# Loading half of the tap weights behind x, and giving the first products of layer 0 banks of their own

## Chip, cores and metric

One core of a Trainium2 chip runs the whole program. The metric is device time in microseconds, the median of several executions; lower is better. The engines are TensorE (PE, with its weight loads as PEld), VectorE (DVE), ScalarE (ACT), GpSimd (POOL) and SyncE (SP, which here only issues DMAs).

## The reference, cut to what matters

The model has two residual layers on an image of 64 x 64 positions with 96 channels. The change touches layer 0 alone. Inside it, the part in question is the input projection, the depthwise 3 x 3 convolution with SiLU, and the first steps of a selective scan in four directions:

```
x = x + L0(groupnorm(x))
x = x + L1(groupnorm(x))

L0(x):
    xz = x @ in_proj_w                    # 96 -> 2 * 192
    x_val, z = xz[..., :192], xz[..., 192:]
    xc = depthwise_conv3x3(x_val) + conv_b
    u = silu(xc)                          # 64 x 64 x 192
    y = scan(u by rows) + scan(reversed) + scan(u by columns) + scan(reversed)
    y = layernorm(y) * silu(z)
    return y @ out_proj_w

scan(u):
    x_dbl = u @ x_proj_w                  # dt (6), B (16), C (16)
    dt = softplus(x_dbl[dt] @ dt_proj_w + dt_proj_b)
    decay = exp(cumsum(dt * A))
    h = decay * cumsum(dt * B * u / (decay + 1e-12))
    return sum_n(h * C) + u * D_skip
```

## The kernel before

**Layout.** Channels lie on partitions, positions along the free axis. The 192 inner channels make two tiles: tile 0 has channels 0 to 127, tile 1 the other 64, which appear twice so that the two halves of the partitions hold two stretches of positions. The image is cut into 8 blocks of 512 positions (`NCH`) and 4 chunks of 1024 (`NSC`). In the scan of layer 0 the factor `decay` falls so fast that only the first positions of each direction contribute (the windows, at most 160 of 192 steps `WT`); the rest of the image needs only the convolution, SiLU and a scaling with `D_skip`.

**Tile 0** folds the projection and the convolution into one matrix product. `load_taps` allocates `wi` (the projection's weights) and `cw` (the nine taps, broadcast to 96 partitions and for both tiles, 2 x 128 columns each). `load_cw` issues the load of `cw` on ACT's queue. In `front`, two GpSimd products (taps 0 to 4 and 5 to 8) turn `cw` into tap times projection weight. A block of convolved output is then nine accumulated matmuls with `cw[:, j, 0:P]` on shifted views of `pad`, the normalized image with a border of zeros. Only these first 128 columns of `cw` are read by a matmul.

**Tile 1** projects first and convolves afterwards: `depthwise` has PE make `px` (helper `project`), ACT copies it to `xz` (chunks 0 and 1) or `xz_later` (chunks 2 and 3), and DVE adds up nine taps per chunk with `scalar_tensor_tensor`, two chunks in turn.

**Order.** All instructions of layer 0 go through the class `Ordered`, which chains those of each engine in program order; its line, L373, is therefore the line of nearly every row of the profile. What order the engines see is thus the order in which the Python code calls them. `run` first loads (`load_x` puts two quarters of `x` on ACT's queue and two on SP's), then calls `front`: 32 transposes on PE into PSUM tiles `pt`, BN statistics on DVE and copies to `x1` on ACT, the group norm's mean and deviation with small products on PE and some products `warm` between them, and the normalization into `pad` and, for the outermost columns, `edge`. DVE does `pad` of block 0, both `edge` parts and `pad` of blocks 1, 2, 4 and 6; ACT does blocks 7, 3 and 5.

Then comes `window_inputs`: the products `pxw` of rows and columns at the image's edges for tile 1 (two matmuls each, in the two halves of a PSUM tile), copied by ACT to `window_work` and convolved by DVE; the products `pw` of tile 0 for the same positions, rows first and then columns; and SiLU of both into `uw`. From here three generators are advanced by a list of steps written out by hand in `run`: `depth` (tile 1), `conv` (tile 0: three matmuls per step, and a finished block `pc` evicted by ACT in the middle of the next) and `work`, which is `windows`: `pdw` (the `x_proj` product, two halves), `dblw` copied out and stored, `pvw` (the product with `dt_proj_w`, two tiles), the logarithm of softplus by quadratics (`wq`, `wacc`), the gates by Exp and Sigmoid, the rows of B and C reloaded from DRAM (`wB`, `wC`), one scan per tile and the sum `wy`. After the list the generators run in turn, joined by `finish`, which applies SiLU and the scaling to each chunk as soon as it is convolved. Layer norm, gating with `z` and the output projection follow, then layer 1.

**PSUM** has eight banks here: `px` and `pv` (two banks each), `wp` (one) and `conv` (three of one bank). Before, `pxw` uses `px` for the rows and `pv` for the columns, every `px` of `depthwise` uses `px`, both `pdw` use `wp`, and both `pvw` use `pv`. A tile that is handed out again under the same tag can be written only when its earlier readers are done.

Of the kernel before, what the change touches and what calls it, by code (L numbers as in the profile page):

```python
# [11 lines left out]
F32 = mybir.dt.float32  # L12
BF16 = mybir.dt.bfloat16
AF = mybir.ActivationFunctionType
ALU = mybir.AluOpType
# [5 lines left out]
C = 96  # L21
# [3 lines left out]
E = R + 2 * NS  # L25
P = 128
# [360 lines left out]
class Layer0:  # L387
# [24 lines left out]
    def load_taps(self, sb):  # L412
        nc = self.nc
        self.wi = sb.tile([C, 2 * P], F32, name="wi_0")
        nc.sync.dma_start(self.wi, self.w_in)
        self.cw = sb.tile([C, 9, 2 * P], F32, name="cw_0")

    def load_cw(self):

        self.nc.scalar.dma_start(  # L420
            self.cw.rearrange("p k d -> p (k d)"),
            self.conv_w.rearrange("o k d -> o (k d)").to_broadcast([C, 9 * 2 * P]),
        )
# [13 lines left out]
    def front(self, sb, ps):  # L437
# [4 lines left out]
        for b in range(NCH):  # L442
            pt = ps.tile([C, NB // P, P], F32, tag="tr", bufs=4, name=f"pt_{b}")
            for j in range(NB // P):
                nc.tensor.transpose(pt[:, j, :], self.xt[:, b * (NB // P) + j, :], k["ident"])
            nc.vector.bn_stats(stats[:, b, :], pt.rearrange("c j p -> c (j p)"))
            nc.scalar.copy(
                free(x1, (n, P), (1, NB // P), at=b * (NB // P)),
                free(pt, (1, P), (P, NB // P)),
            )  # L450
            if b == 0:
                self.load_cw()
        for some in (slice(0, 5), slice(5, 9)):
            n = some.stop - some.start
            at = self.cw[:, some, :]
            nc.gpsimd.tensor_tensor(at, at, free(self.wi, (0, n), (1, 2 * P)), ALU.mult)

# [34 lines left out]
    def window_inputs(self, sb, ps):  # L492
# [8 lines left out]
        for cols in range(2):  # L501
            px = ps.tile([P, 2, NB], F32, tag=("px", "pv")[cols], name=f"pxw_{cols}")
            for i, first in enumerate((0, side)):
                lines = (side, 2)[i]
# [11 lines left out]
                at = 2 * (cols * n + first * (W + 2))  # L516
                nc.scalar.copy(xw[:, at : at + width], px[:, i, 0:width])
        depth = self.depthwise(self.conv_sb, ps)
# [18 lines left out]
        for cols in range(2):  # L537
            pw = ps.tile([P, 2, side, H], F32, tag="conv", bufs=3, name=f"pw_{cols}")
            for j in range(9):
# [9 lines left out]
                nc.tensor.matmul(pw, self.cw[:, j, 0:P], at, start=(j == 0), stop=(j == 8))  # L549
            if cols == 0:  # L550
                next(depth)
            for back in range(2):
# [51 lines left out]
    def depthwise(self, sb, ps):  # L604
# [4 lines left out]
        def project(c):  # L609
            px = ps.tile([P, 2, NB], F32, tag="px", name=f"px_{c}")  # L610
            for i in range(2):
# [14 lines left out]
        for c in range(2):  # L626
            xz.append(project(c))
            yield

# [6 lines left out]
        for pair in range(0, NSC, 2):  # L636
            for j in range(9):
                for c in range(pair, pair + 2):
# [7 lines left out]
                    else:  # L646
                        nc.vector.scalar_tensor_tensor(
                            out, at, self.taps[:, j : j + 1], out, ALU.mult, ALU.add
                        )
                if j in (4, 8) and len(xz) < NSC:  # L650
                    xz.append(project(len(xz)))
# [27 lines left out]
    def windows(self, sb, ps):  # L679
# [10 lines left out]
        for h in range(2):  # L690
            pd = free(
                ps.tile([P, NB], F32, tag="wp", name=f"pdw_{h}")[0:E, :], (WT, 2), (1, WT)
            )
# [9 lines left out]
        for t in range(2):  # L703
            pv = ps.tile([P, 2, NB], F32, tag="pv", name=f"pvw_{t}")
            for h in range(2):
# [404 lines left out]
    def run(self, load):  # L1110
        nc, tc, side = self.nc, self.tc, WT // H
        with ExitStack() as st:
# [8 lines left out]
            with tc.tile_pool(name="front0", bufs=1) as fr, tc.tile_pool(  # L1121
# [8 lines left out]
                nc.gpsimd.memset(self.edge, 0.0)  # L1130
                nc.gpsimd.memset(self.zero, 0.0)
                self.load_later(res, sb)
                self.front(fr, ps)
                next(load)
# [8 lines left out]
            for step in (  # L1143
                depth, work, depth, conv, work, work, depth, conv, work, depth, conv, depth,
                work, conv, work, work, conv, work, work,
            ):
                next(step)
# [933 lines left out]
```

## Time and profile before

| what | us |
|---|---|
| median of three runs | 605.26 (604.91 to 607.9) |
| the profiled execution's own time | 603.7 |
| its span on the core | 602.0 |
| busy in the span: PE / DVE / ACT / POOL | 497.4 / 506.5 / 323.0 / 357.7 |
| busy from 16 to 124 us: PE / DVE / ACT / POOL | 101.84 / 86.71 / 58.88 / 20.64 |
| first product `pxw` starts | 17.33 |
| layer 1 begins (its load of tap weights is issued) | 171.3 |

The times within the profile count from the start of the span. A row of the timeline gives start, duration, engine, source line and instruction with `out<-in`, the shape, the number of instructions merged into the row, and in brackets how long the engine had been idle before the row and what it was waiting for. A row of the table of stages gives a stretch, its length, the busy time of PE, PEld, DVE, ACT and POOL with the number of instructions, the clock that PE was granted (1.00 is full speed), the share of the DMA engines that was busy, and GB/s.

### The profile page before, as it was taken

The numbers are of one execution on the slowest core, as the hardware profiler recorded it, in microseconds if no ns is written. First come the engines' busy times: TensorE is split into PE (matmuls) and PEld (weight loads), VectorE is DVE, ScalarE is ACT, GpSimd is POOL, SyncE is SP. The second block draws the span as 40 slices with busy tenths as digits, with TensorE's granted clock in tenths as the row PEclk, the third lists the DMA queues.
The fourth block names the chain that finished last, engine by engine and source line by source line (L and its number), as shares of the span: only waits on it lengthen the run. The fifth ranks groups of instructions, "written<-read, shape, count | busy, mean of one in ns | idle before, by whom it ended". The sixth has DMA issues, their size and how long they took to land.

```text
span 602.0 us, 4796 instructions
## 1 busy us (share of the span) xinstructions
PE 497.4 (83%) x1363; PEld 196.9 (33%) x1363; DVE 506.5 (84%) x465; ACT 323.0 (54%) x491; POOL 357.7 (59%) x205
## 2 busy tenths in 40 slices
PE   5798999997988997995689987878997566998583
PEld 3253444535842332331113322112332101433111
DVE  6974899934851899999999999999899999899991
ACT  5325599358834857582576765275665335333410
POOL 5326010003420298866697879888787896689961
PEclk9688799997999799996779989787997967897967
DMA  6100730000010816762675637674565585465911
GB/s 178 31 2 10 211 123 0 0 1 1 2 26 13 240 62 182 251 178 72 145 231 172 211 114 175 164 215 145 183 195 144 138 213 193 139 233 176 223 41 33
DMA packets 29734, 76.20 MB, mean 127 GB/s; under 512 B 10880, under 2 KB 11292, under 8 KB 29346
## 3 DMA queue, kind: packets, MB, share of 16 engines
q1 hardware_dynamic: 29186, 73.83, 42.5%
q10 hardware_dynamic: 512, 1.97, 1.1%
q8 instruction: 13, 0.21, 0.1%
q14 instruction: 23, 0.19, 0.1%
HBM read 69.37 MB, written 2.25 MB: 119 GB/s over the span
## 4 chain that ended last, share of the span: by engine, by line
DVE 37%; PE 20%; issue 8%; ACT 5%; POOL 1%; DMA 1%; DVEq 0%; POOLq 0%; ACTq 0%; SPq 0%
DVE h L373 20%; PE y L373 9%; DVE f L373 8%; DVE acc L373 5%; PE f L373 2%; PE pd L373 2%; PE po L373 2%; ACT f L373 2%; PE pv L373 1%; ACT q L373 1%; DVE dt L373 1%; PE f_pc L373 1%; ACT e L373 1%; ACT dA L373 1%; PE f_pd L373 1%
## 5 line engine op out<-in xcount | busy, mean ns | idle before, releaser
L373 POOL TENSOR_TENSOR C<-C,h 128x1024 f32<-128x1024 f32 x96 | 233.2, 2441 | 41.6 <-issue 14.3
L373 DVE TENSOR_TENSOR_SCAN h<-dA,last,f 128x1024 f32<-128x1024 f32 x57 | 133.8, 2347 | 7.5
L373 PE MATMUL y<-C,ident 128*128 128x512 f32 x256 | 131.6, 637 | 6.6 <-POOL C L373 6.4
L373 DVE TENSOR_TENSOR f<-f,w 128x1024 f32<-128x1024 f32 x76 | 92.2, 1214 | 6.3 <-PE f L373 5.9
L373 PE MATMUL f<-parts,pick 96*128 96x512 bf16 x144 | 49.1, 426 | 49.3 <-DVE h L373 49.3
L373 ACT ACTIVATE dA<-dt,A 128x1024 f32<-128x1024 f32 x76 | 86.3, 1143 | 3.1 <-DVE h L373 1.6
L373 PEld LDWEIGHTS y<-C,ident 128*128 128x128 f32 x256 | 50.1, 201 | 62.5 <-issue 42.4
L373 PE MATMUL pc<-pad,cw 96*128 96x512 f32 (+1 forms) x144 | 62.1, 594 | 0.0
L373 PE MATMUL y<-C,both 128*64 128x512 f32 x128 | 47.9, 841 | 7.6 <-POOL C L373 7.6
L373 POOL TENSOR_TENSOR B<-B,w 128x1024 f32<-128x1024 f32 x20 | 47.6, 2378 | 1.2 <-DMA B<-bc_dram 1.1
L373 ACT COPY last<-h 128x1 f32<-128x1 f32 x72 | 13.5, 187 | 64.4 <-DVE h L373 64.3
L373 PEld LDWEIGHTS <-pick 96*128 96x128 bf16 x144 | 10.3, 100 | 109.6 <-DVE h L373 68.1
L373 DVE TENSOR_TENSOR_SCAN h<-dA,f 128x1024 f32<-128x1024 f32 x19 | 43.4, 2286 | 2.2
L373 ACT ACTIVATE q<-e,quad 128x512 f32<-128x512 f32 (+1 forms) x24 | 27.3, 1145 | 31.2 <-DVE acc L373 30.9
L373 DVE SCALAR_TENSOR_TENSOR acc<-q,acc 128x512 f32<-128x512 f32 (+1 forms) x18 | 42.7, 2370 | 1.6 <-ACT q L373 1.3
L373 ACT ACTIVATE f<-dt,A 128x1024 f32<-128x1024 f32 x20 | 22.3, 1114 | 35.3 <-DVE h L373 26.9
L373 PEld LDWEIGHTS pc<-pad,cw 96*128 96x128 f32 x144 | 29.2, 206 | 32.5 <-issue 30.7
L373 PE MATMUL pc<-xn,cw 96*64 96x512 f32 (+1 forms) x84 | 33.5, 684 | 5.1 <-ACT u L373 4.8
L373 DVE TENSOR_TENSOR_SCAN h<-f,last,B 128x1024 f32<-128x1024 f32 x15 | 35.0, 2332 | 0.0
L373 POOL TENSOR_TENSOR rest<-dbl,parts 96x1024 f32<-96x1024 f32 (+1 forms) x5 | 11.1, 2215 | 37.9 <-ACT parts L373 37.8
L373 POOL TENSOR_SCALAR ln_small<-ln_small 128x4 f32<-128x4 f32 x2 | 0.5, 235 | 52.4 <-DVE ln_small L373 52.4
L373 ACT ACT_TABLE_LOAD x17 | 21.8, 1283 | 2.0 <-PEq L2071 1.7
(212 smaller groups left out, 732.5 us busy)
## 6 DMA issues: line engine op xcount, KB each, us to landing
C<-bc_dram SPq DMA_DIRECT2D x64, 512.0 KB, 3.9
C<-bc_dram SPq DMA_DIRECT2D x64, 256.0 KB, 4.2
B<-bc_dram SPq DMA_DIRECT2D x12, 512.0 KB, 5.4
B<-bc_dram SPq DMA_DIRECT2D x16, 256.0 KB, 4.4
dt<-dt SPq DMA_DIRECT2D x16, 128.0 KB, 2.3
w<-w SPq DMA_DIRECT2D x16, 128.0 KB, 2.3
wB<-rows_dram SPq DMA_DIRECT2D x1, 1472.0 KB
wC<-rows_dram SPq DMA_DIRECT2D x1, 1472.0 KB
```

The source lines that it names most:

```text
L373: ins = it(*args, **kw)
```

## The change

`cw` keeps only tile 0's half, 9 taps of 128 columns, loaded with nine pieces of 128 values for each partition; the load is issued before `load_later`, that is, ahead of `front`, and one GpSimd product follows there instead of two in `front`. In `window_inputs` both matmuls of a `pxw` tile come before both copies. The four `px` of `depthwise` take the tags `px` and `pv` in turn, the second `pdw` takes a `conv` bank, and the two `pvw` take `px` and `pv`. `depthwise` projects chunks 0 and 1 in one step, ahead of `pw`, and chunks 2 and 3 together after tap 4 of the first pair; `depth` then has one step more in the list and is advanced in other places. In the order of instructions on the engines this moves one `px` of PE ahead of the first `pw`, one ahead of the first `pc`, with it the copy of the last `xz_later` on ACT ahead of `pvw`'s readers, and four of DVE's taps on `xz_later` ahead of `wacc`.

```diff
@@ load_taps, load_cw
-        self.cw = sb.tile([C, 9, 2 * P], F32, name="cw_0")
+        self.cw = sb.tile([C, 9, P], F32, name="cw_0")
...
+        w = self.conv_w
         self.nc.scalar.dma_start(
-            self.cw.rearrange("p k d -> p (k d)"),
-            self.conv_w.rearrange("o k d -> o (k d)").to_broadcast([C, 9 * 2 * P]),
+            self.cw, bass.AP(w.tensor, w.offset, [[0, C], [2 * P, 9], [1, P]])
         )
@@ front
-            if b == 0:
-                self.load_cw()
-        for some in (slice(0, 5), slice(5, 9)):
-            n = some.stop - some.start
-            at = self.cw[:, some, :]
-            nc.gpsimd.tensor_tensor(at, at, free(self.wi, (0, n), (1, 2 * P)), ALU.mult)
@@ window_inputs
+            copies = []
             for i, first in enumerate((0, side)):
...
-                nc.scalar.copy(xw[:, at : at + width], px[:, i, 0:width])
+                copies.append((xw[:, at : at + width], px[:, i, 0:width]))
+            for to, of in copies:
+                nc.scalar.copy(to, of)
...
-            if cols == 0:
-                next(depth)
@@ depthwise
-            px = ps.tile([P, 2, NB], F32, tag="px", name=f"px_{c}")
+            px = ps.tile([P, 2, NB], F32, tag=("px", "pv")[c % 2], name=f"px_{c}")
...
         for c in range(2):
             xz.append(project(c))
-            yield
+        yield
...
-                if j in (4, 8) and len(xz) < NSC:
+                while j == 4 and len(xz) < NSC:
                     xz.append(project(len(xz)))
@@ windows
-                ps.tile([P, NB], F32, tag="wp", name=f"pdw_{h}")[0:E, :], (WT, 2), (1, WT)
+                ps.tile(
+                    [P, NB], F32, tag=("wp", "conv")[h], bufs=(1, 3)[h], name=f"pdw_{h}"
+                )[0:E, :], (WT, 2), (1, WT)
...
-            pv = ps.tile([P, 2, NB], F32, tag="pv", name=f"pvw_{t}")
+            pv = ps.tile([P, 2, NB], F32, tag=("px", "pv")[t], name=f"pvw_{t}")
@@ run
+                self.load_cw()
                 self.load_later(res, sb)
+                nc.gpsimd.tensor_tensor(
+                    self.cw, self.cw, free(self.wi, (0, 9), (1, P)), ALU.mult
+                )
                 self.front(fr, ps)
...
             for step in (
-                depth, work, depth, conv, work, work, depth, conv, work, depth, conv, depth,
-                work, conv, work, work, conv, work, work,
+                depth, work, depth, conv, work, work, conv, depth, work, depth, conv, depth,
+                depth, work, conv, work, work, conv, work, work,
             ):
```

## The prediction

> **What bounds the kernel now.** All of the change lies in layer 0, which ends near 172 us of a span of 602.0 in the profiled execution. So I first asked the timeline which engine carries layer 0 from the first products (17.3 us) to the end of the convolution. The last lines of that stage, ACT and then DVE:
>
> ```profile
> 119.03 0.69 ACT L373 ACTIVATE v<-pc,vec 128x512 f32<-128x512 f32 x1 [3.73 <-PE pc L373]
> 123.87 0.53 ACT L373 ACTIVATE v<-pc,vec 128x320 f32<-128x320 f32 x1 [4.16 <-PE pc L373]
> 126.76 2.39 DVE L373 TENSOR_TENSOR v<-v,wy 128x192 f32<-128x192 f32 x8 [7.08 <-ACT v L373]
> ```
>
> Columns: start, duration (us), engine, instruction, then in brackets the idle time before it and what ended it. DVE sat idle for 7.08 us until ACT had finished the last chunk, and ACT had waited 4.16 us for PE's last convolution product `pc`. Everything after hangs on that point: PE's convolution sets it, not the window scans on DVE (done at 119.7). Next the table of stages on core 0, with PE's granted clock behind POOL's column:
>
> ```profile
> 17.20:20.60 3.40, 1.64 (x5) 0.59 (x4) 3.40 (x2) 2.11 (x4) 3.40 (x2) 1.00 0.32 66
> 20.60:24.00 3.40, 1.66 (x2) 0.50 (x2) 3.40 (x6) 0.01 (x1) 1.29 (x1) 0.53 0.16 35
> 24.00:34.20 10.20, 9.67 (x20) 4.63 (x21) 9.54 (x17) 1.57 (x3) 0.00 (x0) 0.50 0.01 2
> 34.20:51.30 17.10, 16.54 (x59) 7.43 (x57) 13.43 (x21) 6.11 (x13) 9.98 (x15) 0.99 0.01 3
> 51.30:54.90 3.60, 2.03 (x8) 1.19 (x8) 0.00 (x0) 1.48 (x2) 3.38 (x5) 1.00 0.04 18
> 54.90:68.30 13.40, 13.40 (x27) 6.34 (x26) 5.44 (x9) 7.84 (x10) 0.00 (x0) 0.50 0.31 74
> 68.30:102.90 34.60, 34.60 (x81) 15.11 (x80) 33.93 (x37) 32.37 (x64) 1.63 (x10) 1.00 0.36 117
> ```
>
> PE is busy nearly throughout, but in two stretches, 20.6 to 34.2 and 54.9 to 68.3, at a clock of 0.50. Each follows a stretch of about 3.5 us in which PE worked only half the time (1.64 of 3.40, 2.03 of 3.60). The same matmul shows it: eighteen `pw` records take 9.20 us from 28.1, mostly in the first stretch, and 6.08 us from 38.5. So a short wait of PE costs here several times its own length. The waits themselves:
>
> ```profile
> 16.59 5.56 DVE L373 TENSOR_SCALAR edge<-x,mean,rstd 96x256 f32<-96x256 f32 x2
> ...
> 18.98 0.71 PE L373 MATMUL pxw<-pad,wi 96*128 96x264 f32 x2 [0.74 <-ACT window_work L373]
> ...
> 22.30 1.66 PE L373 MATMUL pxw<-edge,wi 96*128 96x396 f32 x2 [2.60 <-DVE edge L373]
> ...
> 24.53 1.25 PE L373 MATMUL pxw<-edge,wi 96*128 96x264 f32 x2 [0.58 <-ACT window_work L373]
> ...
> 46.67 1.60 PE L373 MATMUL pdw<-uw,w_x 128*38 128x384 f32 x4 [0.56 <-ACT dblw L373]
> ...
> 54.19 1.82 PE L373 MATMUL pvw<-dblw,dtw 6*128 6x320 f32 x4 [1.57 <-ACT wdt L373]
> ```
>
> The second `pxw` product waits for the copy of the first, though it fills another half of the tile; the second `pdw` and `pvw` wait for the readers of their predecessor's tile. The 2.60 us belong to `edge`: two DVE operations on 256 elements in 5.56 us, where `pad` with 512 takes 0.54. POOL's product with the tap weights runs beside them (16.24 to 21.88, in two records of 3.18 and 2.51), and each `edge` record (3.10 and 2.55) ends about 0.27 us after one of POOL's. And one long wait on DVE:
>
> ```profile
> 62.70 0.55 DVE L373 TENSOR_SCALAR v<-xz_later,taps,vec 128x512 f32<-128x512 f32 x1 [11.46 <-ACT xz_later L373]
> ```
>
> **What the Trainium skill says.** "SBUF — State Buffer", section "SBUF: two separate sides": DVE and GpSimd share a port pair, an exclusive lock held for a whole instruction, taken by DVE operations in a two-port mode or with two SBUF inputs. The `edge` durations agree. BN statistics read from PSUM should be free of it, and the trace agrees: eight of them at 0.61 us each beside nothing, and later 4 in 1.14 us beside a POOL product (155.84, POOL busy 155.43 to 157.24) as in 1.16 without. "TensorE: Matmul & The Clock Gate", Part 1: the clock halves after an idle window of about 3.4 us and recovers after one busy window. The trace agrees on the half clock and the window, but a half-idle window was enough, and it took 13.6 and 13.4 us, four windows, to come back; I use the measured lengths. "DMA: Bandwidth & Descriptors", Specifications: 512 bytes is the least size at full rate, which is just what the new load has; no row before shows such pieces.
>
> **The change part by part.**
>
> Tap weights. Before, the load is issued at 9.45 behind the first `x` copy and lands 6.6 us later, 864 KB. Now 432 KB are issued behind ACT's `root` activation, which ends at 6.13. ACT idles from there to 9.45, so the issue (0.34 us) costs nothing; the queue carries `x`, whose traffic has dropped from 401 to 25 GB/s by 8 to 10 us, so `x` isn't delayed. Flight: half of 6.6 as the lower bound, all of 6.6 if pieces of 512 bytes go at half the rate; I take 4.5, landing at 10.7 (9.4 to 12.8). POOL's product has 1152 elements at the old 2.45 ns (2505 ns for 1024), 2.8 us, so it ends at 13.5 (12.2 to 15.6), beside BN statistics. At the late end it could hold the small two-input operations at 14.6 for 1 us; I take 0. Nothing on POOL waits behind it before `uw` at 29. SP's `w_x` issue, which waits 4.3 us for the old load, comes sooner too; no other queue is passed.
>
> `edge` then takes 0.35 us each (half of 0.54 and some for its stride): done at 17.3 instead of 22.15, and DVE's four `pad` pieces (1.91) at 19.2 instead of 24.0.
>
> Own banks. With both matmuls ahead of both copies, PE goes from 17.33 without a stop: four `pxw` products of 1320 columns at 1.74 ns (6.0 us for nine of 384) end at 19.6. The first `px` needs ACT's copies of `pxw` 0: ACT's `pad` pieces end at 18.56, copies at 19.4. The second `px`, now in the other tile, needs the copies of `pxw` 1 (20.6), and PE comes to it at 20.9. So PE has no wait where it lost 3.9 us, the half-idle window at 17.2 to 20.6 is gone, and I let the first slow stretch go.
>
> PE's timetable at full clock, each length from the row before: `px` twice 1.26, to 22.1; `pw` twice 6.0, to 34.1 (POOL's weights are there since 13.5); `pdw` 1.3, to 35.5; the second `pdw` has its own bank but needs the second half of `uw` from ACT, 1.35 us behind `pw` as before, so PE waits 0.1 and goes on to 37.1; `px` twice 2.5, to 39.7; three `pc` 1.8, to 41.5; `pvw` twice 1.1, to 43.7 (`dblw` is ready at 37.6, and the second no longer waits); six `pc` 3.2, to 46.9. A full chunk takes 7.73 (ACT received two at 111.30 and 119.03), the short last one 4.84: four chunks to 77.9, two thirds of the next to 83.0, `wy` 5.5 (102.94 to 108.47) to 88.5, the rest 2.6 + 7.73 + 4.84, to 103.7. Before: 123.8. **That is 20.1 us sooner**: about 6.1 of waits, 12 of half clock, the rest hand-overs around the waits.
>
> What is late next? ACT and DVE with the windows. DVE starts on `window_work` at 19.5 instead of 23.9; 5.7 + 5.7, then the `xz` taps 12.0, to 42.9. `in_proj` of tile 1 (both `xz_later`) comes from PE at 38.4 and 39.7, so the 11.46 us wait goes, and ten operations on it (1.0 + 5.5) end at 49.4; POOL's `uw` may hold one for 0.6. ACT: `pvw` is ready at 42.6 and 43.7, two activations each, a table load, two Exp to 48, `wq` to 48.8. So `wacc` starts at 49.9 instead of 65.81, 15.9 sooner, and the chain behind it (logarithm, Exp, sigmoid, scans), as long as before, with it: `wg` for `wy` at 97.26 - 15.9 = 81.4, which PE needs at 83.0; the eviction of the bank that PE reuses at 77.9, at 91.7 - 15.9 = 75.8; DVE free at 103.8, while PE and ACT let it start at 126.76 - 20.1 = 106.7. The scans' loads follow `dblw`, 11 us sooner; they end at 80.6 before, and `wC` is first read at 95.1, so they stay hidden. All margins are 1.5 to 3 us, and PE still ends last.
>
> Sum: 603.7 (span 602.0 and 1.7 around it) - 20 = 583.7. The median of the three runs shown, 605.26, is 1.6 above this execution: 585.3.
>
> **The rivals.**
> A, as above: 585.3; 582 to 589, since a 6 us slow stretch early in layer 1 (194.9 to 201.2) may fall otherwise, worth up to 3 either way, and the margins may leak 2.
> B, one slow stretch stays, around `pdw` and `pvw`, where PE's products are narrow and the 0.1 us wait may be 1: half of 13.5 us is 6.7, 592. For it: a half-idle window was enough twice. Against: my timetable has under 0.5 us of waits from 17 to 104.
> C, the lock isn't what slows `edge` (its strided read is): PE still waits until 22.3, the first slow stretch stays, and only the 0.58, 0.56 and 1.57 us and the second stretch's 6.7 go: 9.4, 596. Against: the ends 0.27 us behind POOL's.
> D, the change doesn't do what it says: the windows' chain or the shared banks give a new wait, and what `xz_later` frees returns as a stall of PE in front of `wy`. That needs the chain 20 us late; no row shows it: 605.
> E, slower: the many pieces make the load late. 864 pieces over 16 DMA engines are 54 each. PE would idle from 22.1 until POOL is done, and go to half clock (6.7 us). With 13.4 us left to lose, the point is weights ready at 35.5, landed at 32.7, 26 us after issue or nearly 0.5 us a piece; landing at 36 gives 608.6. Against: 864 KB took 6.6 us.
>
> **How the numbers follow.** Chances: A 0.68, B 0.15, C 0.10, D 0.03, E 0.04. Predicted is A's 585.3. The range 582 to 597 holds A, B and C less their edges. A measurement here tells about 0.5%, 3 us, from no change: faster 0.93 (A, B, C), same 0.03, slower 0.04.
>
> **What would show it.** `edge` at 0.3 to 0.4 us each and POOL's `cw` over by 16; no wait of `pxw`, `pdw` or `pvw` on ACT over 0.3; PE's clock at 1.00 from 17 to 104; the last `pc` received at about 104; the DVE wait on `xz_later` gone; layer 1 as long as before. The prediction fails if a half clock remains in 17 to 104, if `cw` lands after 15, or if DVE reaches its last window sums later than ACT.

## The result and the profile after

| what | before | after |
|---|---|---|
| median, us | 605.09 (601.65 to 607.9, 4 runs) | 582.62 (581.31 to 586.54, 4 runs) |
| ratio after to before, 95% interval | | 0.9642 [0.9571, 0.9713] |
| the profiled execution, us (its span) | 603.7 (602.0) | 586.54 (584.8) |
| the last `pc` reaches ACT | 123.87 | 105.53 |
| layer 1 begins | 171.33 | 153.55 |
| layer 1 to the end of the span | 430.7 | 431.3 |

The time fell by 22.5 us, a ratio of 0.9642. The profiled execution happens to be the longest of after's four, so the two traces differ by only 17.2 us. When the last convolution product arrives the lead is 18.3 us; the way from there to layer 1 (48.0 us, before 47.5) and layer 1 itself give 1.1 of it back. Medians and ratios, here and below, leave out executions more than 1.5% slower than their kernel's fastest; the traces of `load_undone` and `banks_undone` are of such executions, so I read waits and stretches from them and not their totals.

The end of the stage in the timeline of the kernel after (start, duration, engine, instruction, idle time before it and what ended it):

```profile
100.69 0.69 ACT L373 ACTIVATE v<-pc,vec 128x512 f32<-128x512 f32 x1 [3.73 <-PE pc L373]
105.53 0.53 ACT L373 ACTIVATE v<-pc,vec 128x320 f32<-128x320 f32 x1 [4.16 <-PE pc L373]
108.42 2.40 DVE L373 TENSOR_TENSOR v<-v,wy 128x192 f32<-128x192 f32 x8 [3.72 <-ACT v L373]
```

PE still ends last: ACT waits for `pc` and DVE for ACT, both 18.34 us sooner than before. DVE's idle time shrank from 7.08 to 3.72, so the windows' chain did not gain as much as PE did. The same timeline at the start of the stage:

```profile
9.54 2.63 POOL L373 TENSOR_TENSOR cw<-cw,wi 96x1152 f32<-96x1152 f32 x1 [1.33 <-DVE stats L373]
...
16.58 1.04 DVE L373 TENSOR_SCALAR edge<-x,mean,rstd 96x256 f32<-96x256 f32 x2
...
17.32 1.35 PE L373 MATMUL pxw<-pad,wi 96*128 96x396 f32 x4
...
18.51 1.27 PE L373 MATMUL pxw<-edge,wi 96*128 96x396 f32 x4
...
31.81 13.01 DVE L373 SCALAR_TENSOR_TENSOR v<-xz,taps,v 128x512 f32<-128x512 f32 x16
...
33.91 3.13 PE L373 MATMUL pdw<-uw,w_x 128*38 128x384 f32 x8
...
37.31 4.32 POOL L373 CAST pick<-state 96x2048 bf16<-96x2048 f32 x3
...
41.17 2.42 PE L373 MATMUL pvw<-dblw,dtw 6*128 6x320 f32 x8
```

POOL's product is over 4 us before `edge` starts, `edge` takes 1.04 us for both parts where it took 5.56, and none of the waits shown of before is left: `pxw`, `pdw` and `pvw` run without a wait. The table of stages (length, busy time of PE, PEld, DVE, ACT, POOL, then PE's clock):

```profile
17.20:20.60 3.40, 3.29 (x15) 1.91 (x16) 3.33 (x8) 2.90 (x6) 0.00 (x0) 1.00 0.10 20
20.60:34.20 13.60, 13.60 (x49) 7.42 (x46) 12.97 (x22) 4.11 (x8) 5.35 (x13) 1.00 0.01 2
34.20:44.60 10.40, 10.40 (x42) 4.80 (x41) 10.40 (x13) 5.47 (x12) 7.28 (x8) 1.00 0.04 12
44.60:48.00 3.40, 3.40 (x7) 2.07 (x7) 3.40 (x7) 3.37 (x6) 0.00 (x0) 0.51 0.05 8
48.00:105.00 57.00, 57.00 (x164) 28.73 (x163) 52.98 (x50) 41.83 (x76) 1.63 (x10) 1.00 0.30 88
```

The 27 us of half clock that stood between 20 and 69 are gone, but for one stretch of 3.4 us, from 44.6 to 48.0. PE had been busy without a break in front of it. I had not expected that, and much of what follows is about it.

### The profile page after: what moved, and what is told of

Read it like the earlier page. It is cut to its first block, busy times and chain, and to the rows that moved or that the text cites. A ratio compares the mean times of both kernels' runs of the same rounds, so it can differ in the third digit from the quotient of the medians.

```text
span 584.8 us, 4794 instructions
## 1 busy us (share of the span) xinstructions
PE 489.0 (84%) x1363; PEld 195.1 (33%) x1363; DVE 504.2 (86%) x465; ACT 322.8 (55%) x491; POOL 353.9 (61%) x204
## 4 chain that ended last, share of the span: by engine, by line
DVE 37%; PE 22%; issue 8%; ACT 5%; POOL 1%; DMA 0%; DVEq 0%; POOLq 0%; ACTq 0%; SPq 0%
DVE h L373 20%; PE y L373 9%; DVE f L373 9%; DVE acc L373 6%; PE f L373 3%; PE pd L373 2%; PE po L373 2%; ACT f L373 2%; PE pv L373 2%; DVE dt L373 1%; ACT q L373 1%; PE f_pc L373 1%; PE pc L373 1%; PE f_pd L373 1%; POOL C L373 1%
## 5 line engine op out<-in xcount | busy, mean ns | idle before, releaser
L373 PEld LDWEIGHTS y<-C,ident 128*128 128x128 f32 x256 | 50.1, 200 | 61.9 <-issue 41.7
L373 PE MATMUL pc<-pad,cw 96*128 96x512 f32 (+1 forms) x144 | 58.5, 567 | 0.0
L373 ACT COPY last<-h 128x1 f32<-128x1 f32 x72 | 13.5, 187 | 64.1 <-DVE h L373 64.0
L373 POOL TENSOR_TENSOR B<-B,w 128x1024 f32<-128x1024 f32 x20 | 47.5, 2377 | 1.5 <-DMA B<-bc_dram 1.4
L373 ACT ACTIVATE f<-dt,A 128x1024 f32<-128x1024 f32 x20 | 22.3, 1114 | 35.3 <-DVE h L373 26.9
L373 PE MATMUL pc<-xn,cw 96*64 96x512 f32 (+1 forms) x84 | 35.3, 722 | 5.5 <-ACT u L373 5.2
L373 PEld LDWEIGHTS pc<-pad,cw 96*128 96x128 f32 x144 | 27.9, 195 | 29.8 <-issue 27.5
```

What stands on the lines that cost most here:

```text
L373: ins = it(*args, **kw)
```

## The experiments

Twelve runs follow, each beside the kernel before. None leaves a part of the computation out; where one adds work, its paragraph says so. "Last `pc`" and "layer 1 begins" are read from each trace as in the table above.

| run | median us | ratio to before, 95% interval | last `pc` | layer 1 begins |
|---|---|---|---|---|
| load_only | 597.4 | 0.9887 [0.9834, 0.9941] | 113.85 | 160.90 |
| load_undone | 590.71 | 0.9764 [0.9721, 0.9807] | 113.53 | |
| inproj_undone | 590.58 | 0.9749 [0.9707, 0.9791] | 107.99 | 158.06 |
| lock_dose | 587.02 | 0.9699 [0.965, 0.9749] | 109.94 | 155.04 |
| half_late | 600.12 | 0.9932 [0.989, 0.9974] | 117.34 | 164.51 |
| pvw_rows | 583.62 | 0.9636 [0.961, 0.9663] | 104.36 | 149.47 |
| pvw_apart | 586.98 | 0.9676 [0.9643, 0.9709] | 104.25 | 156.67 |
| wy_late | 585.28 | 0.966 [0.962, 0.9699] | 99.94 | 150.94 |
| banks_undone | 593.55 | 0.9814 [0.9769, 0.9859] | 119.45 | |
| rows_wy | 584.44 | 0.9651 [0.9613, 0.9689] | 99.25 | 150.04 |
| after_again | 582.90 | 0.9636 [0.9596, 0.9676] | 105.53 | 150.63 |
| inproj_rows | 584.79 | 0.9663 [0.9628, 0.9698] | 105.03 | 152.45 |

### The load: alone, undone, and half undone

`load_only` is the kernel before with the load part of the diff alone (its core below); `load_undone` is the kernel after with the same lines turned round.

```diff
-        self.cw = sb.tile([C, 9, 2 * P], F32, name="cw_0")
+        self.cw = sb.tile([C, 9, P], F32, name="cw_0")
...
+                self.load_cw()
                 self.load_later(res, sb)
+                nc.gpsimd.tensor_tensor(
+                    self.cw, self.cw, free(self.wi, (0, 9), (1, P)), ALU.mult
+                )
```

> The kernel before with the load part alone: half of cw, its load ahead of front, one GpSimd product there; banks and in_proj order as before. Lock theory (GpSimd's product holds the port that DVE's edge needs): edge takes about 0.5 us each instead of 2.8, PE gets its column pxw at about 19.6 instead of 22.3, the half-clock stretch 20.6 to 34.2 is gone or short, the second at pvw stays as in the kernel before. Last pc at ACT about 115 (before 123.87): some 596 us. Stride theory (edge is slow by its own strided read): edge stays at 2.8 us, nothing gained, 604 to 606. A theory in which banks are what matters: the waits of pxw on ACT (0.74 and 0.58) keep the first half-clock stretch even with a quick edge, 602.

> The changed kernel with the load part undone: cw whole, loaded behind the first copy of x, two GpSimd products in front; own banks and the new in_proj order stay. Lock theory: edge is at 2.8 us each again, PE waits for it until 22.3, the half-clock stretch of 13.6 us from about 20.6 is back, pvw's waits stay away; last pc at ACT about 114 to 116 against 105.53, so about 591 us. If the load part is worth nothing, 582.6. If the parts work only together, near 602.

Both times came as my theory said, 597.4 and 590.71. In the timeline of `load_only`:

```profile
16.58 1.07 DVE L373 TENSOR_SCALAR edge<-x,mean,rstd 96x256 f32<-96x256 f32 x2
...
18.98 0.71 PE L373 MATMUL pxw<-pad,wi 96*128 96x264 f32 x2 [0.75 <-ACT window_work L373]
...
20.94 0.71 PE L373 MATMUL pxw<-edge,wi 96*128 96x264 f32 x2 [0.58 <-ACT window_work L373]
```

The load part removes the wait on `edge` and nothing else; the waits on shared banks stay. They did not start the first slow stretch here: PE's clock is 1.00 from 17.2 to 47.5, and half only from there to 57.7. That is 10 us of the last `pc`, and a ratio of 0.9887 in the medians. Part of it may be where these waits fell in time. The clock changes only at the borders of windows of 3.4 us (shown further down); here the two waits lie in two windows, in `banks_undone`, below, the same two (0.74 and 0.58) lie in one, and there half clock followed. The windows in question, `load_only` first, with PE's busy time behind the length:

```profile
16.75:20.16 3.41, 2.56 (x8) 0.97 (x6) 3.37 (x8) 2.56 (x5) 0.00 (x0) 1.00 0.13 21
20.16:23.57 3.41, 2.83 (x13) 1.27 (x13) 3.17 (x6) 1.45 (x3) 0.00 (x0) 1.00 0.00 0
```
```profile
18.05:21.46 3.41, 2.09 (x7) 0.92 (x6) 3.33 (x7) 2.03 (x5) 0.00 (x0) 1.00 0.08 15
21.46:31.70 10.24, 9.41 (x24) 3.79 (x24) 9.62 (x17) 3.08 (x4) 0.00 (x0) 0.50 0.01 2
```

In `load_undone` the lock shows, but not at `edge` as I had expected (its timeline, POOL and DVE):

```profile
16.25 5.19 POOL L373 TENSOR_TENSOR cw<-cw,wi 96x1280 f32<-96x1280 f32 x2 [8.04 <-DMA cw<-in_cw]
```
```profile
16.41 2.74 DVE L373 SCALAR_TENSOR_TENSOR shift<-mean,rstd 96x1 f32<-96x1 f32 x1
19.07 2.65 DVE L373 TENSOR_SCALAR pad<-x,mean,rstd 96x512 f32<-96x512 f32 x1
21.65 1.03 DVE L373 TENSOR_SCALAR edge<-x,mean,rstd 96x256 f32<-96x256 f32 x2
```

POOL came 0.16 us ahead of DVE's `shift`, so it was `shift`, a single column, and then `pad` that took 2.7 us each, and `edge` was free. Whichever of these operations DVE has next pays for POOL's product, and pays for it whole. Half clock came back too, from 22.3 to 25.7 and from 49.6 to 56.4, and not as the one stretch of 13.6 us that I had expected.

`half_late` asks whether half the bytes would do without the earlier issue: `cw` halved, but issued where it was, with one product in `front`. Against before, beside the halved tile and its load:

```diff
             if b == 0:
                 self.load_cw()
-        for some in (slice(0, 5), slice(5, 9)):
-            n = some.stop - some.start
-            at = self.cw[:, some, :]
-            nc.gpsimd.tensor_tensor(at, at, free(self.wi, (0, n), (1, 2 * P)), ALU.mult)
+        nc.gpsimd.tensor_tensor(self.cw, self.cw, free(self.wi, (0, 9), (1, P)), ALU.mult)
```

> The kernel before with half of cw, but loaded where it was, behind the first copy of x, and one GpSimd product in front instead of two. Separates half from early. Lock theory: the load lands near 13 to 14, the product ends by 16.8, edge is blocked by at most 1 us and the result is that of load_only, 592 to 599 us, last pc at ACT 113 to 118. Rival (the early issue is what pays): edge ends after 19 and the time is near that of the kernel before, 603 to 606.

It gave 0.9932 [0.989, 0.9974] with a median of 600.12, between the two forecasts; the last `pc`, at 117.34, is as my theory had it, and `edge` ends after 19 as the rival had it, but not by the rival's cause. In its timeline POOL, then DVE:

```profile
14.12 2.61 POOL L373 TENSOR_TENSOR cw<-cw,wi 96x1152 f32<-96x1152 f32 x1 [5.92 <-DMA w_x<-in_w_x]
```
```profile
14.41 0.15 DVE L373 TENSOR_SCALAR mean<-gn 96x1 f32<-96x1 f32 x1 [0.42 <-PE gn L373]
14.60 2.14 DVE L373 TENSOR_TENSOR dev<-mv,mean 96x1 f32<-96x1 f32 x1
...
18.72 1.05 DVE L373 TENSOR_SCALAR edge<-x,mean,rstd 96x256 f32<-96x256 f32 x2
```

`edge` is free at 1.05, but the product now lies on the group norm: `dev`, 0.15 us otherwise, ends at 16.74, just behind POOL at 16.73, while `mean`, which reads PSUM, passes beside POOL in 0.15. Everything after is 2.1 us late, and the last `pc` comes 3.5 us after that of `load_only`. So half the bytes alone is less than the whole load part in these traces; the intervals of the two ratios overlap, so the times alone don't show it. Whether the earlier issue would do with all the bytes was not run. From before's lengths (6.6 us of flight, 5.64 of product) I estimate that an issue at 3.98 would end that product near 16.2, ahead of `edge` but right on the group norm's operations. I had named this cost in the prediction ("could hold the small two-input operations at 14.6") and taken it as 0, rightly only because the load came early.

### The lock itself

The rival C held that `edge` is slow by its strided read. `lock_dose` is the kernel after with two more POOL products into a tile that nobody reads, released at the moment when DVE comes to `pad` and `edge`; this adds work and changes nothing else. Ahead of `pad` and `edge`:

```diff
+        for _ in range(2):
+            nc.gpsimd.tensor_tensor(
+                self.junk, self.cw, free(shift, (0, 9), (0, P)), ALU.mult
+            )
```

> The changed kernel with two more GpSimd products of the tap weights' size, started by the group norm's shift at 16.3 us and written to a tile that nothing reads: work is added, the result is the same. Lock theory: each edge operation takes 2.5 to 3 us again and ends right behind a GpSimd product, PE waits for edge from 18.5 to about 22.5, 4 us, and loses half of one to four clock windows of 3.4 us on top: last pc at ACT 111 to 117 against 105.53, 588 to 594 us. Stride theory or no lock: edge stays at 0.5 us each, the last pc at 105.5, 582.6 us.

```profile
16.38 4.50 POOL L373 TENSOR_TENSOR junk<-cw,shift 96x1152 f32<-96x1152 f32 x2 [3.87 <-DVE shift L373]
```
```profile
16.61 4.53 DVE L373 TENSOR_SCALAR edge<-x,mean,rstd 96x256 f32<-96x256 f32 x2
```
```profile
21.29 2.54 PE L373 MATMUL pxw<-edge,wi 96*128 96x396 f32 x4 [2.59 <-DVE edge L373]
```

The same two `edge` operations, with the same stride, take 4.53 us beside POOL and 1.04 without: C falls. PE's wait of before (2.60) is back as 2.59, half clock follows it from 21.1 to 28.0, and the last `pc` is 4.4 us late: more than the wait, as the prediction had read it from the trace of before. The size was a miss: 109.94 and 587.02 us instead of 111 to 117 and 588 to 594, as I had put the wait at 4 us, and as after's own stretch behind `pvw` did not come in this execution. The Trainium skill, "SBUF — State Buffer", section "SBUF: two separate sides", says that the lock is held for a whole instruction, and the trace agrees: DVE's second `edge` ends at 21.14, just behind POOL's second product at 20.88.

### The own banks

`banks_undone` is the kernel after with the tiles of before for `px`, `pvw` (below) and `pdw`, and each `pxw` copy right behind its matmul again.

```diff
-            px = ps.tile([P, 2, NB], F32, tag=("px", "pv")[c % 2], name=f"px_{c}")
+            px = ps.tile([P, 2, NB], F32, tag="px", name=f"px_{c}")
...
-            pv = ps.tile([P, 2, NB], F32, tag=("px", "pv")[t], name=f"pvw_{t}")
+            pv = ps.tile([P, 2, NB], F32, tag="pv", name=f"pvw_{t}")
```

> The kernel after, with the banks of the kernel before: each pxw copied right behind its matmul, every px in one tile, both pdw in one bank, both pvw in one tile; early half load and the new order of in_proj stay. If the own banks carry their part: pxw waits return (0.7 and 0.6 us), the second px of each pair waits for ACT's copies of the first (1 to 1.5 us each), the second pdw 0.6, the second pvw 1.5: 5 to 6 us of waits before 50 us, and at least one half-clock stretch more than after has there (1.7 us for each 3.4), so the last pc reaches ACT at 112 to 116 instead of 105.5, 590 to 596 us. Rival, the banks are worth only their waits (no new half clock): last pc near 110, 587 to 589. Rival, they were worth nothing once the load is early: pc within 1.5 us of 105.5 and 582 to 586.

Its timeline, PE:

```profile
19.26 0.71 PE L373 MATMUL pxw<-pad,wi 96*128 96x264 f32 x2 [0.74 <-ACT window_work L373]
...
21.22 1.04 PE L373 MATMUL pxw<-edge,wi 96*128 96x264 f32 x2 [0.58 <-ACT window_work L373]
...
25.50 2.47 PE L373 MATMUL px<-pad,wi 96*64 96x330 f32 x8 [0.83 <-ACT xz L373]
...
43.75 1.60 PE L373 MATMUL pdw<-uw,w_x 128*38 128x384 f32 x4 [0.56 <-ACT dblw L373]
...
47.50 1.33 PE L373 MATMUL px<-pad,wi 96*64 96x330 f32 x8 [0.89 <-ACT xz_later L373]
...
53.49 2.50 PE L373 MATMUL pvw<-dblw,dtw 6*128 6x320 f32 x4 [1.57 <-ACT wdt L373]
```

Six waits, 5.17 us in all, as expected, and half clock from 21.5 to 31.7 and from 52.2 to 62.4. The undoing costs 0.0172 in the ratio against after, some 10 us: twice the waits, so the rival that the banks are worth their waits alone (587 to 589) falls. The last `pc` of this execution came later (119.45) than the 112 to 116 I had expected; the median, 593.55, fits. That the clock takes the other half in the executions behind the median too is inferred from this one trace. By the medians the banks are the largest of the three parts; the intervals of `banks_undone` and `load_undone` overlap.

### In_proj's order, and the stretch after `pvw`

`inproj_undone` is the kernel after with the old order: one `px` per step, the last `px` only after tap 8, and the old list of steps.

```diff
             xz.append(project(c))
-        yield
+            yield
...
-                while j == 4 and len(xz) < NSC:
+                if j in (4, 8) and len(xz) < NSC:
...
+            if cols == 0:
+                next(depth)
...
-                depth, work, depth, conv, work, work, conv, depth, work, depth, conv, depth,
-                depth, work, conv, work, work, conv, work, work,
+                depth, work, depth, conv, work, work, depth, conv, work, depth, conv, depth,
+                work, conv, work, work, conv, work, work,
```

> The changed kernel with the old in_proj order (chunk 1 behind the first pw, chunks 2 and 3 in two steps); load and banks as changed. My theory: PE's work is only reordered and its clock is kept, so the last pc at ACT stays within 1 us of 105.5; but DVE waits again for xz_later, up to 7 us, so the window chain ends nearer to PE or behind it, and DVE's last sums begin 0 to 3 us later: 583 to 586 us. Rival (sooner in_proj is where most of the gain comes from): 590 or more.

A miss: 590.58 instead of 583 to 586, which is the rival's time. PE's part of its timeline, and two rows of its table of stages:

```profile
40.41 2.42 PE L373 MATMUL pvw<-dblw,dtw 6*128 6x320 f32 x8
...
44.69 2.47 PE L373 MATMUL px<-pad,wi 96*64 96x330 f32 x8
```
```profile
41.10:44.60 3.50, 3.50 (x13) 1.93 (x11) 3.50 (x4) 2.81 (x4) 3.39 (x4) 1.00 0.03 10
44.60:51.40 6.80, 6.75 (x17) 3.39 (x17) 3.52 (x7) 4.73 (x7) 1.10 (x2) 0.51 0.03 5
```

PE does not wait, and yet the stretch at half clock is twice as long as in after: the last `px` (1.33 us at full clock) takes 2.47 in it. So the order matters to PE's clock. What DVE was to gain by the new order it did not gain: `wacc` begins at 51.06 here and at 50.96 in after. What precedes the stretch in both kernels is a window full of `pvw`, products with 6 rows of weights. `pvw_rows` changes only that: 38 rows instead of 6, the other 32 with zero weights (they multiply the rows of B and C that lie in `dblw` anyway); this adds a small fill of the weights' tile, and moves later lines by one.

```diff
-    lay["dt_w"] = sb.tile([R, 2, P], F32, name=f"dtw_{name}")
-    nc.sync.dma_start(lay["dt_w"], dt_w)
+    lay["dt_w"] = sb.tile([E, 2, P], F32, name=f"dtw_{name}")
+    nc.gpsimd.memset(lay["dt_w"], 0.0)
+    nc.sync.dma_start(lay["dt_w"][0:R], dt_w)
...
-                    dblw[0:R, 2 * h : 2 * h + 2, 0:WIN], start=True, stop=True,
+                    dblw[0:E, 2 * h : 2 * h + 2, 0:WIN], start=True, stop=True,
```

> The changed kernel with the second operand of pvw widened from 6 to 38 rows (the weights of the other rows are zero, so the result is the same; one memset of GpSimd is added). Theory that PE's clock follows the rows in use and not the busy time: the half-clock stretch behind pvw (44.6 to 48.0, with PE busy throughout) is gone, last pc at ACT at 103.8 instead of 105.53, some 581 us. If 38 rows are still too few, or the columns or the narrow outputs of pdw and px are what counts: a stretch of 3.4 us or more remains and the time is 582.6.

`pvw_apart` leaves the 6 rows, but puts three `pc` between the two `pvw`, by the list of steps alone.

```diff
-                depth, work, depth, conv, work, work, conv, depth, work, depth, conv, depth,
+                depth, work, depth, conv, work, conv, work, conv, depth, work, depth, depth,
```

> The changed kernel with three of the convolution's matmuls put between the two pvw products (only the hand-written list of steps differs). Theory that a clock window filled with products of 6 rows counts as idle: no window of 3.4 us is filled with them now, the half-clock stretch at 44 to 48 is gone or not longer than 3.4 us, last pc at ACT 103.8 to 105.5, 580 to 583 us. If the clock falls whenever such products occur at all: 582.6 or a little more.

PE in the timeline of `pvw_rows`, then the stages of `pvw_rows` and of `pvw_apart`:

```profile
41.69 2.42 PE L374 MATMUL pvw<-dblw,dtw 38*128 38x320 f32 x8
```
```profile
44.60:48.00 3.40, 3.40 (x13) 2.26 (x12) 3.40 (x7) 3.37 (x5) 0.00 (x0) 1.00 0.04 7
```
```profile
44.60:48.00 3.40, 3.40 (x12) 1.99 (x11) 3.40 (x7) 2.34 (x3) 0.00 (x0) 1.00 0.04 8
...
105.00:119.00 14.00, 12.69 (x28) 4.20 (x28) 5.09 (x27) 6.81 (x12) 0.36 (x2) 0.63 0.00 1
```

With 38 rows `pvw` takes the same 2.42 us, and there is no half clock there; nor is there when the two are apart. The last `pc` came at 104.36 with a start of the products 0.5 us later (17.84), and at 104.25, as expected. But both times are misses: 583.62 and 586.98 instead of some 581 and of 580 to 583, and neither can be told from after's. In the profiled execution of `pvw_apart` half clock came back from 108.5 to 118.8 and ate the gain.

`inproj_rows` joins the old order and the 38 rows, to see whether the miss was that stretch. Against `inproj_undone`:

```diff
-    lay["dt_w"] = sb.tile([R, 2, P], F32, name=f"dtw_{name}")
+    lay["dt_w"] = sb.tile([E, 2, P], F32, name=f"dtw_{name}")
+    nc.gpsimd.memset(lay["dt_w"], 0.0)
...
-                    dblw[0:R, 2 * h : 2 * h + 2, 0:WIN], start=True, stop=True,
+                    dblw[0:E, 2 * h : 2 * h + 2, 0:WIN], start=True, stop=True,
```

> The old order of in_proj once more, with pvw's contraction widened from 6 to 38 rows by zero rows. If the old order costs its time because the half clock falls on the last px (it follows pvw in the same narrow stretch), the stretch of 6.8 us at 44 to 51 goes, the last pc comes at 104 to 105 instead of 108.0 and the time falls from 590.6 to 583 to 586. Rival, the old order costs through DVE (its waits of 3.3 us on xz_later and of 6 us before the last sums) or through where later stretches fall: the stretch at 44 to 51 goes, but the time stays at 588 to 592. Rival, the 64 columns of px bring the half clock, not pvw's 6 rows: the stretch stays, pc at 108, 588 to 592.

```profile
45.05 1.33 PE L374 MATMUL px<-pad,wi 96*64 96x330 f32 x8
```
```profile
44.60:51.40 6.80, 6.75 (x24) 3.24 (x23) 3.53 (x6) 5.08 (x7) 1.46 (x3) 1.00 0.03 5
```

The same order, the same busy 6.75 us, but 24 products instead of 17 in it, at full clock. The last `pc` is at 105.03 and the time 584.79, as expected and not to be told from after's. DVE's wait of 3.27 us on `xz_later`, which the old order brings, is still there and costs nothing visible. So the new order of in_proj is worth some 6 us in this kernel, and with wider `pvw` nothing that can be measured. Only about half of that is seen behind `pvw`: between the two traces the last `pc` differs by 3.0 us, and the other 2.7 come between it and layer 1 (50.1 us and 47.4), where `inproj_undone` ran at half clock from 113.0 to 119.8 and from 133.5 to 136.9, and `inproj_rows` from 124.7 to 131.5. Whether that half belongs to the order as well isn't shown.

**Is it the rows, or where the windows fall?** Reading the clock in slices of 0.5 us, I found that within one trace all changes of the clock lie on one grid of 3.413 us (before: 20.8, 34.4, 54.9, 68.6, 143.7 and 150.5), and that the grid lies elsewhere in each execution. So a kernel that moves `pvw` by 0.5 us, or only the next execution, may escape a stretch by chance. The grid of each trace tells how much of the 2.42 us of `pvw` fell into one of its windows (worked out from the times of the two; `pvw_rows` has no change of the clock between 12.5 and 172.9, but these two, 47 windows apart, give its grid):

| trace | rows | most of `pvw` in one window, us | half clock next |
|---|---|---|---|
| after, after_again, wy_late | 6 | 2.4 | 3.4 us |
| load_undone | 6 | 2.1 | 6.8 us |
| inproj_undone | 6 | 1.5 | 6.8 us |
| pvw_apart | 6 | 1.3 | none |
| lock_dose | 6 | 1.2 | none |
| inproj_rows | 38 | 2.0 | none |
| pvw_rows | 38 | 1.5 | none |
| rows_wy | 38 | 1.4 | none |

PE was busy throughout each of these windows (in the traces with 6 rows that aren't in the table PE also waited in the window). With 6 rows, 1.5 us or more of `pvw` in a window brought half clock, and 1.3 or less did not. For the rows speak two traces, `inproj_rows` with 2.0 us and none, and, on the border, `pvw_rows`; in `rows_wy` the grid alone could explain it. So the rows are likely, but two traces don't show it.

### What else could win, and the spread

`wy_late` moves the second `wy` product of PE behind the convolution; `rows_wy` is that with the 38 rows of `pvw_rows`.

```diff
-            y1 = ps.tile([P, 2, NB], F32, tag="pv", name="wy_1")
-            self.sum_window1(y1, g[1], classes[1][0])
...
+        y1 = ps.tile([P, 2, NB], F32, tag="pv", name="wy_1")
+        self.sum_window1(y1, g[1], classes[1][0])
         self.add_window0(y)
         self.add_window1(y1)
```

> The changed kernel with the sums wy, 5.5 us of PE in the middle of the sixth block, moved behind the convolution. They are needed only by the last window sums. Theory that PE's convolution still sets the end of this stage: last pc at ACT 5.5 us sooner, near 100, but then DVE, free at 104.7, becomes the bound: DVE's eight sums begin near 105 instead of 108.4 and 579 to 580 us result. If the tail behind it (z projection on PE) is the bound, nothing: 582.6.

> pvw_rows and wy_late together: pvw widened with zero rows, and wy behind the convolution. If both effects add: no half clock before 100 us, last pc at 98 to 99, DVE then the bound, layer 1 begins near 149 (153.6 after), and 580 to 583 us. Rival: layer 1 begins earlier, but the total stays with after's (582 to 586), since the part behind 150 us varies by more with the granted clock than what is won.

> The kernel after once more, on this chip beside the two others: 582 to 587 us, last pc at 105.5 and a half clock of 3.4 us right behind pvw (44 to 48) again if that stretch belongs to the kernel; if it was an accident of the one execution, it is gone or lies elsewhere and pc is at 103.8.

In the timeline of `wy_late`:

```profile
99.94 0.53 ACT L373 ACTIVATE v<-pc,vec 128x320 f32<-128x320 f32 x1 [4.16 <-PE pc L373]
...
104.14 3.15 DVE L373 TENSOR_TENSOR v<-v,wy 128x192 f32<-128x192 f32 x10
```

The last `pc` is 5.6 us sooner, and DVE now goes through without its idle 3.7 us: the bound has moved to DVE's windows, and PE reaches the next stage at the same time (105.28, after 105.33), since `wy` stands there instead. The time, 585.28, misses the 579 to 580 expected and fits the rival, that what follows on PE is the bound; so does `rows_wy` with 584.44. Neither kernel can be told from after; I found no version that beats it.

`after_again` is the kernel after once more, beside these two. Its last `pc` comes at 105.53 again, and the stretch stands again, at 44.3 to 47.8. But layer 1 begins 2.9 us sooner than in the first execution. Two windows of the grid in each, after first:

```profile
123.05:126.46 3.41, 1.57 (x12) 1.10 (x11) 1.77 (x11) 3.40 (x8) 0.74 (x1) 1.00 0.00 0
126.46:129.87 3.41, 2.56 (x9) 2.35 (x10) 1.40 (x7) 3.41 (x9) 2.30 (x2) 0.50 0.00 0
```
```profile
122.84:126.25 3.41, 1.75 (x12) 1.28 (x12) 1.69 (x11) 3.40 (x7) 0.53 (x1) 1.00 0.00 0
126.25:129.66 3.41, 2.35 (x14) 2.18 (x15) 1.93 (x13) 3.41 (x10) 2.29 (x2) 1.00 0.00 0
```

It is the same stretch of the same work. The grid lies 0.2 us earlier in the second; the first window holds 1.75 us of PE's work instead of 1.57, and the next runs at full clock: 14 products instead of 9. But busy time is not what decides. `pvw_apart` and `inproj_rows` each have a window with 2.10 us of the product `pz`, one wait of 1.31 us in it:

```profile
105.09:108.50 3.41, 2.10 (x7) 0.46 (x7) 1.30 (x5) 3.41 (x6) 0.00 (x0) 1.00 0.00 0
```
```profile
107.65:111.06 3.41, 2.10 (x8) 0.79 (x8) 2.98 (x14) 2.90 (x7) 0.00 (x0) 1.00 0.00 0
```

The first, of `pvw_apart`, was followed by half clock up to 118.8; the second was not. Eight traces have such a window. Where the wait ended 2.4 us or more behind the window's start (`pvw_apart`, `inproj_undone`, `load_undone`, `banks_undone`), half clock followed; where it ended by 2.1 us (before, `load_only`, `half_late`, `inproj_rows`), it did not. Whether the place of the wait is the cause wasn't tested.

From the last `pc` to layer 1 the traces of this study take 45.1 us (`after_again`, `pvw_rows`, `lock_dose`) to 52.5 (`banks_undone`), while layer 1 takes 430 to 431 in nearly all (`rows_wy` 432.8, `half_late` 433.9). In these traces that tail is most of the spread of a few us between executions, and it hides gains of 1 to 3 us.

## Why the prediction was right, step by step

Forecast 585.3 and A, measured 582.62: right in its sum and, but for two terms, in its steps. One of its own signs of being wrong did come, though: half clock remained between 17 and 104. And the closeness of the sum is in part luck: the last `pc` came 1.8 us later than forecast, while the median fell by 2.5 us more than the 20.

- **Tap weights.** Landing was put at 10.7. POOL's product ran from 9.54 to 12.17 (expected to end at 13.5). Two errors met: ACT issued the load already at 3.98, though it stands behind `root` (5.50 to 5.70) in ACT's order, and the flight was at most 5.6 us instead of 4.5. The pieces of 512 bytes cost no more than the upper bound that I had set for them, and E had no ground: the margin before PE needs the weights (22.1) is 10 us.
- **`edge`** took 0.52 each instead of 0.35. The end at 17.6 instead of 17.3 reached nobody. That it was the lock was right (`lock_dose`).
- **Own banks.** PE's timetable held to 0.4 us up to `pvw`: `pw` at 22.09 (22.1), `pdw` at 33.91 (34.1), `pc` from 39.35 (39.7), `pc` again from 43.51 (43.7).
- **The clock** is the term that was mis-sized. I had let all half clock go, since no wait was left. One stretch of 3.4 us at 44.6 stayed and costs 1.7 us. It accounts for nearly all of the difference at the last `pc` (105.53 instead of 103.7), and DVE's last sums (108.42 instead of 106.7) follow. Rival B had named the place ("where PE's products are narrow"), but took a wait as the cause and a size of 6.7 us. It came without a wait, in a window filled with `pvw`, at a quarter of the size.
- **The windows' chain.** `wacc` began at 50.96 instead of 49.9. The 11.46 us wait went as said, but the taps on `xz` took 14.0 us and not 12.0. Of the 16 scaled sums that took 13.01 us (10.93 before), three took 2.37, 1.09 and 1.09 where the others take 0.74: they lie beside three POOL operations, the casts to `pick`, of 2.29, 1.06 and 1.06, and each ends some 0.5 us behind one of them. Before, these ran from 51.8 to 54.8, while DVE idled in the very wait that is now gone. So the lock had moved to other work, which the prediction hadn't priced (it gave POOL's `uw` 0.6 us here and the casts nothing). DVE was free at 104.7 instead of 103.8. It cost nothing, as PE came later still.
- **Layer 1** was as long as before: 431.3 and 430.5 against 430.7.
- **The sum.** 20 us were promised at the last `pc`; 18.3 came there. The profiled executions differ by 17.2 (after) and 20.8 (after_again), depending on the tail, the work between the last `pc` and layer 1; the medians by 22.5. Before's trace had half clock there too (143.7 to 150.5). Whether the medians gained beyond 18 by a better tail wasn't tested. (The stretch in layer 1 that A's range names lies from 194.9 to 201.7 in before's trace, 6.8 us and not 6; it changes nothing.)
- **How the gain divides.** By cause, the split at the last `pc` held roughly. The five waits that the prediction shows (6.05 us) went. PE was busy for 24.7 us of the slow stretches in its table of stages, so half clock had cost 12.4, and 1.7 of that stayed: 10.7 gained, by this estimate, and some 1.6 of the 18.3 are left for the rest. By parts of the edit, the load alone brings 0.0113 in the ratio (7 us), and undoing the load, the order or the banks costs 0.0122, 0.0107 and 0.0172 (7.4, 6.5 and 10.4 us): 24 in all, where the whole change gained 22. The intervals are too wide to tell these apart. But undoing any one of the three brought a stretch of half clock back, or made one longer: one wait, or one window of narrow products, can be enough.

## What to carry to other kernels

Follow a short wait of PE to the clock that comes after it before pricing it: here 5.2 us of waits cost 10, and an order of instructions without any wait of PE cost 6, of which 2.5 were there by the last `pc`. Where DVE shows one operation several times its usual length, look for a POOL instruction that ends when it does; moving POOL's work frees that operation, but check which DVE operations then lie beside it. And when a gain is no larger than the spread that the clock makes in a later stage, compare the traces up to that stage, and profile the same kernel twice before believing a total.

## What the runs showed of the hardware

- The Trainium skill, "TensorE: Matmul & The Clock Gate", Part 1, calls the clock's window free-running. The traces agree: one grid of 3.413 us in each, at another place in each execution, and the two executions of after part by 0.2 us of it.
- PE's busy time in a window does not decide what follows. A window with 1.57 us of PE's work was followed by half clock, in before (17.4 to 20.8) and in after; one with 1.75 was not (`after_again`). But of eight windows with 2.1 us of the same products, four were followed by half clock, those in which PE's wait lay late, and four were not (two are shown under the spread). And fully busy windows with 1.5 us or more of 6-row products were followed by it as well. What is measured instead of busy time stays open. Two traces with 38 rows point to the rows, but these can't be all of it: the eight windows of 2.1 us hold products of 96 rows.
- Coming back took one window in after, two in `inproj_undone` (44.7 to 51.6), three in `load_only` (47.5 to 57.7) and four before the change (54.9 to 68.6), with PE busy all the while. The same page gives one busy window, which agrees with the first alone.
- The lock between DVE and POOL stretches an operation on one column as much as one on 512: `shift` took 2.74 us and `dev` 2.14, where each takes 0.15 without; `pad`, on 512, took 2.65.
- A DMA needn't wait for all activations that stand ahead of it on its engine: the load of `cw` was issued at 3.98, as `A` began (3.97), with a table load (4.21 to 5.49) and `root` still to come.
